# Two-pass attention: the second pass started 13 steps, not 16, behind the first

## Chip, cores, metric

The kernel runs on one core of one Trainium2 chip. The metric is the device time in microseconds (us) of one execution.

## What is computed

The reference is a chain of four blocks over an input of 8 batches of 512 rows and 128 columns, each with a residual addition and a layer normalisation: an attention with 16 heads of 8 columns and a distance bias, a gated feed-forward with block-wise quantisation, a second 16-head attention without bias, and two layers of windowed attention with a feed-forward. The change lies in the two 16-head attentions. Each of these is

```
qkv    = x @ W_qkv.T + b_qkv                     # (8, 512, 384), split in 16 heads of 8
scores = q @ k.T / sqrt(8)  (+ bias, first attention only)   # (8, 16, 512, 512)
probs  = softmax(scores)
x      = layernorm(x + (probs @ v) @ W_out.T + b_out)
```

## The kernel before

`body` runs `attention(0, ...)`, `ffn0()`, `attention(1, ...)` and `ffn1()` in that order. All is in float32 in the core's own memory, and one attention works on it batch by batch.

**Units and steps.** A batch has four units (g = 0 to 3), each of two pairs of heads. A unit needs two passes over its scores. The first pass finds the maximum of each row: for each block of 128 query rows and each pair of heads, two matmuls write scores to `s_ps`, and VectorE (DVE) reduces them to `m` (line 239). The second pass computes the scores again, transposed and with the row's maximum already subtracted, in `t_ps`; ScalarE (ACT) takes the exponential `e` (line 245); `values` multiplies by v and a column of ones, into `av`. The maximum is subtracted inside the matmul: row 63 (and 127) of the q operand holds it, against a row of -1 in the k operand. A unit takes NU = 8 steps in each pass. In the loop over steps, `step(u, i, v, k)` does step i of the first pass of one unit and step k of the second pass of an earlier one, which is LAG steps behind. So the first LAG steps hold the first pass alone, the last ones the second pass alone, and all others both.

**What hangs on the steps.** A table `todo` says which further functions run after which step; the order on TensorE (PE) is the order in which they are written, as matmuls are kept in program order. With s = 8n the first step of unit n, and z = s + LAG:

- `shift`, after step s + 9: PE transposes the maxima (`m_ps`), ACT copies them (`mt`, line 253), and GpSimd (POOL) issues two small DMAs (`q<-mt`, line 257) that put them into rows 63 and 127 of q. `t_ps` of the unit, from step z on, reads these rows.
- `values`, after steps z + 3 to z + 10; at the end ACT copies `av` to `avs` (line 274).
- `divide`, after step z + 12: PE transposes `avs` (`o_ps`), DVE divides by the sum (lines 282, 284).
- For the last unit of a batch, `end_o` after z + 15 (transpose, copy to `oT`) and `end_y` after z + 18: output projection `y_ps`, addition and statistics on DVE (lines 94 to 99), then `layernorm` on POOL (lines 104, 105, 116).
- The next batch's preparation, on the first pass's own count of steps (32 to a batch): `begin_x` after step 22, `begin_qk` after 24 (q) and 26 (k), `begin_v` after 20. `begin_qk` projects (`qk_ps`), ACT scales (lines 162, 164), POOL splits the result in two parts (`parts`, lines 167, 168), and SyncE (SP) writes them to a scratch area in DRAM (`far`, line 172). `load_qk` reads them back into the operand layout of `q` and `k` in 16 DMAs for each half of the batch (line 184), listed after steps 6, 8, 18 and 20; these write over the rows of the batch before the last one, and so wait for the last `t_ps` that reads them.

**Buffers.** q and k operands are held twice (even and odd batches). In PSUM, `s_ps` has two buffers of two banks, `av` one bank, and one pool of three banks (`p_t`) serves `t_ps` (two at each step) as well as every transpose and projection.

**Names.** A helper records the matmuls, so that PE's instructions of the attentions show as lines 126 and 127, and the tile names tell them apart.

Of the kernel before, what the change touches and what calls it, by code (L numbers as in the profile page):

```python
# [20 lines left out]
NT = S // P  # L21
# [19 lines left out]
def body(ctx, tc, x, consts, rows, wa0, wa1, acols, bo, wf, wqkv, wo, w1, w2, cols, b2r, qs, ks, out):  # L41
# [79 lines left out]
    def attention(li, alibi, qs_, ks_, late=None):  # L121
# [6 lines left out]
        with ExitStack() as st:  # L128
# [176 lines left out]
                add_and_stats(work, ps, xs, b, 0, NT)  # L305
                layernorm(work, b)

            LAG, NU = 16, 2 * NT
            todo = {}
            later = lambda s, f, *a: todo.setdefault(s, []).append((f, a))  # L310
            batch, units = [{} for _ in range(B)], []
# [480 lines left out]
    with tc.tile_pool(name="ops", bufs=1) as ops:  # L792
        qs_, ks_ = ([ops.tile([P, 8, S], F32R, name=f"{n}{i}") for i in range(2)] for n in "qk")
        for i in range(2):
            nc.vector.memset(qs_[i].bitcast(F32), 0.0)
            nc.gpsimd.memset(ks_[i].bitcast(F32), 0.0)

        def constant_rows(i, start):
            for j in range(2):
                for t, at, src in ((ks_[i], 63, rowk[16:17]), (qs_[i], 32, rowq), (ks_[i], 32, rowk[0:16])):  # L800
                    n = src.shape[0]
                    start(
                        out=t[64 * j + at : 64 * j + at + n].bitcast(F32),
                        in_=src.bitcast(F32).unsqueeze(1).broadcast_to([n, 8, S]),
                    )

        def first_late():
            constant_rows(1, held)
            load_late()

        constant_rows(0, nc.sync.dma_start)
        attention(0, True, qs_, ks_, first_late)
        for i in range(2):
            for j in range(2):
                nc.gpsimd.memset(ks_[i][64 * j + 32 : 64 * j + 48].bitcast(F32), 0.0)
        ffn0()
        attention(1, False, qs_, ks_)
# [98 lines left out]
```

## Time and profile before

| what | value |
|---|---|
| time, median of three runs | 2050.5 us (2046.76 to 2053.12) |
| profiled execution, its own time | 2052.7 us |
| its span in the profile | 2050.9 us |
| busy: PE, DVE, ACT, POOL | 1712.4, 1459.0, 1168.8, 829.0 us |
| first attention, first to last reduction `m` | 39.1 to 498.6 us |
| first attention, first to last exponential `e` | 76.5 to 521.8 us |
| second attention, first to last reduction `m` | 746.5 to 1137.7 us |
| second attention, first to last exponential `e` | 767.0 to 1157.8 us |

Busy time is the time in which an engine worked on an instruction; the profile's span runs from the first to the last instruction, and the execution's own time adds what lies around it. PEclk is the granted clock of PE in tenths. In a timeline each line has start, length, engine, source line, operation, output and inputs, shapes and number; in brackets stand the engine's idle time before it and what ended it. "SPq" is SP's queue issuing DMAs.

### The profile page before, as it was taken

Reading aid. Unit: us, or ns where it says so; the run is one execution under the profiler, and the core shown is the slowest. Engines: PE = TensorE matmul, PEld = TensorE weight load, DVE = VectorE, ACT = ScalarE, POOL = GpSimd, SP = SyncE. Lnnn points to the kernel's source line nnn. Section 1 sums busy time; section 2 is a strip of 40 time slices with the busy share of each in tenths; the row PEclk is TensorE's granted clock in tenths of the full one; section 3 lists DMA queues with packets and bytes.
Section 4 is the critical chain, followed back from the end, with each engine's and each line's share of the span. In section 5 each row is a group of like instructions: output and inputs, shape, how many; then the busy total and the mean of one; then the engine's idle time right before and its main releaser. Section 6 shows DMA issues by size and latency. Waiting matters only on the chain.

```text
span 2050.9 us, 41924 instructions
## 1 busy us (share of the span) xinstructions
PE 1712.4 (83%) x16277; PEld 981.8 (48%) x16293; DVE 1459.0 (71%) x2612; ACT 1168.8 (57%) x2749; POOL 829.0 (40%) x880
## 2 busy tenths in 40 slices
PE   1899999999476559999999757888988888888893
PEld 0445455555254424444444324556556555656562
DVE  2677777776588648888889356777777777777752
ACT  0376777777232217877778515566665566655650
POOL 3402222213445451222221434555555555666653
PEclk6699999999787659999999869999999999999997
DMA  5722222310000033333320001111111111111110
GB/s 115 185 54 64 62 52 57 64 23 2 12 1 0 0 97 79 66 65 64 71 63 2 22 16 24 30 31 33 30 32 34 33 32 32 35 35 32 29 30 21
DMA packets 91640, 88.68 MB, mean 43 GB/s; under 512 B 45825, under 2 KB 57473, under 8 KB 91442
## 3 DMA queue, kind: packets, MB, share of 16 engines
q1 hardware_dynamic: 86752, 85.00, 19.1%
q8 instruction: 129, 2.11, 0.4%
q0 software_dynamic: 4096, 0.54, 0.2%
q14 instruction: 69, 0.57, 0.1%
q10 hardware_dynamic: 594, 0.47, 0.1%
HBM read 41.33 MB, written 18.87 MB: 29 GB/s over the span
## 4 chain that ended last, share of the span: by engine, by line
PE 23%; DVE 19%; ACT 15%; POOL 3%; issue 2%; DMA 1%; SPq 1%; ACTq 0%; POOLq 0%; DVEq 0%
ACT pw L466 8%; PE av L126 6%; PE s_ps L126 5%; DVE t L567 4%; DVE r L563 4%; DVE ss L571 3%; PE t_ps L126 3%; DVE m L627 3%; ACT sq L466 2%; PE qk_ps L464 2%; ACT e L245 1%; DVE nrm L590 1%; PE qk_ps L126 1%; DVE u L742 1%; PE p_ps L465 1%
## 5 line engine op out<-in xcount | busy, mean ns | idle before, releaser
L239 DVE TENSOR_REDUCE m<-s_ps 128x2 f32<-128x1024 f32 x512 | 624.2, 1225 | 207.1 <-PE s_ps L126 203.0
L245 ACT ACTIVATE e<-t_ps 128x512 f32<-128x512 f32 x1024 | 555.8, 595 | 185.4 <-PE t_ps L126 175.2
L126 PE MATMUL av<-e,va 128*32 128x256 f32 x4096 | 328.6, 393 | 10.4 <-ACT avs L274 10.3
L466 ACT ACTIVATE pw<-sp,m,nrm 128x128 f32<-128x128 f32 x512 | 226.5, 461 | 183.7 <-DVE m L629 183.0
L126 PE MATMUL s_ps<-k,q 63*128 63x512 f32 x1024 | 266.9, 515 | 48.3 <-DMA k<-far 24.0
L126 PE MATMUL t_ps<-q,k 64*128 64x512 f32 x1024 | 249.0, 449 | 0.0
L257 POOL DMA_DIRECT2D q<-mt x128 | 68.4, 538 | 437.7 <-ACT mt L253 437.7
L126 PEld LDWEIGHTS s_ps<-k,q 63*128 63x128 f32 x1024 | 100.3, 190 | 242.2 <-issue 153.9
L640 POOL TENSOR_TENSOR pw<-pw,den 128x1024 f32<-128x1024 f32 x64 | 121.2, 1894 | 211.3 <-DVE den L639 169.1
L574 POOL TENSOR_TENSOR r<-r,t 128x1024 f32<-128x1024 f32 x64 | 151.0, 2359 | 97.5 <-DVE t L567 95.1
L563 DVE TENSOR_TENSOR r<-qk_ps,tab 128x512 f32<-128x512 f32 x128 | 87.3, 682 | 103.0 <-ACT sq L466 103.0
L464 PE MATMUL qk_ps<-wqkv_s,hT 128*128 128x512 f32 x256 | 136.3, 659 | 16.7 <-DVE t L567 15.9
L126 PEld LDWEIGHTS t_ps<-q,k 64*128 64x128 f32 x1024 | 122.9, 189 | 20.7 <-ACT e L245 10.6
L126 PEld LDWEIGHTS av<-e,va 128*32 128x32 f32 x4096 | 81.8, 108 | 104.1 <-issue 68.8
L465 PE MATMUL p_ps<-cst,pw 128*128 128x128 f32 x512 | 76.3, 284 | 55.1 <-DVE xs L705 31.1
L466 ACT ACTIVATION_READ_ACCUMULATOR pw<-sp,m,nrm 128x1 f32 x512 | 106.1, 207 | 0.0
L126 PEld LDWEIGHTS <-sel 64*128 64x128 bf16 x2048 | 66.8, 97 | 76.4 <-issue 46.6
L467 ACT COPY v<-v_ps 128x512 f32<-128x512 f32 x64 | 37.6, 587 | 105.5 <-PE v_ps L464 105.5
L567 DVE TENSOR_TENSOR t<-qk_ps,tab 128x256 f32<-128x256 f32 x256 | 95.4, 414 | 0.0
L671 DVE COPY pT<-p_ps 128x512 f32<-128x512 f32 x128 | 84.2, 686 | 15.3 <-PE p_ps L465 14.6
L465 PEld LDWEIGHTS p_ps<-cst,pw 128*128 128x128 f32 x512 | 55.8, 142 | 72.3 <-DVE xs L705 25.3
L167 POOL CAST parts<-x 128x512 fp32r<-128x512 f32 x32 | 19.4, 607 | 170.3 <-ACT x L162 166.4
(161 smaller groups left out, 3234.3 us busy)
## 6 DMA issues: line engine op xcount, KB each, us to landing
far<-parts SPq DMA_DIRECT2D x64, 256.0 KB
q<-far SPq DMA_DIRECT2D x256, 64.0 KB
k<-far SPq DMA_DIRECT2D x256, 64.0 KB
ve<-v SPq DMA_DIRECT2D x112, 128.0 KB
xn<-in_x SPq DMA_DIRECT2D x8, 256.0 KB
q<-mt POOLq DMA_DIRECT2D x128, 4.0 KB, 2.9
hn<-xs SPq DMA_DIRECT2D x16, 128.0 KB
out<-xn SPq DMA_DIRECT2D x8, 256.0 KB
```

What stands on the lines that cost most here:

```text
L126: mm = lambda *a, **k: tc.keep_in_program_order(nc.tensor.matmul(*a, **k))
L239: nc.vector.tensor_reduce(u["m"][:, :, pp, blk], both, AX.X, ALU.max)
L245: nc.scalar.activation(e, ts[j], AF.Exp, scale=float(SLOPES[2 * vp + j]) if alibi else 1.0)
L257: nc.gpsimd.dma_start(out=q[at : at + 1, 2 * g : 2 * g + 2, :].bitcast(F32).rearrange("o a (c t) -> o (a c) t", t=P), in_=mt[8 * j : 8 * j ...
L464: mm = lambda *a, **k: tc.keep_in_program_order(nc.tensor.matmul(*a, **k))
L465: tr = lambda *a, **k: tc.keep_in_program_order(nc.tensor.transpose(*a, **k))
L466: act = lambda *a, **k: tc.keep_in_program_order(nc.scalar.activation(*a, **k))
L563: nc.vector.tensor_tensor(heads(r[:, n]), heads(ps[:, n]), cos.unsqueeze(1).broadcast_to([P, HEADS, DH]), ALU.mult)
L567: nc.vector.tensor_tensor(heads(t2[:, n])[:, :, a : a + 32], heads(ps[:, n])[:, :, 32 - a : 64 - a], sin[:, a : a + 32].unsqueeze(1).broad ...
L574: nc.gpsimd.tensor_tensor(r, r, t2, ALU.add)
L640: nc.gpsimd.tensor_tensor(pw.rearrange("p s r k -> p (s r) k"), pw.rearrange("p s r k -> p (s r) k"), den.rearrange("p s r -> p (s r)").un ...
L671: nc.vector.tensor_copy(h["pT"][:, s], ps)
```

## The change

The lag of the second pass behind the first is 13 steps instead of 16, in both attentions. All that is counted from z (values, divide, end_o, end_y) moves with it; what is counted from s stays. With 16, a multiple of the eight steps of a unit, the second pass stood at the same step within its unit as the first; with 13 it stands five steps on.

```diff
-            LAG, NU = 16, 2 * NT
+            LAG, NU = 13, 2 * NT
             todo = {}
             later = lambda s, f, *a: todo.setdefault(s, []).append((f, a))
...
             for n in range(B * G):
...
                 s, z = n * NU, n * NU + LAG
                 later(s + 9, shift, units[n])
                 later(z + 12, divide, units[n])
                 for blk in range(NT):
                     for part in range(2):
                         later(z + 2 * blk + 3 + part, values, units[n], blk, part)
```

## Prediction, made before the changed kernel ran

> **What bounds the kernel now.** I read the page first, by stages. In part 2 each digit is a fortieth of the span, 51 us. The attentions are the stretches of nines in the PE row (100 to 520 us and 780 to 1160 us), at full clock:
>
> ```profile
> PE   1899999999476559999999757888988888888893
> PEclk6699999999787659999999869999999999999997
> ```
>
> The busy time by stretches says the same in numbers (columns: stretch, its length, then busy time and instructions of PE, PEld, DVE, ACT, POOL, then clock, DMA share, GB/s):
>
> ```profile
> 100.00:500.00 400.00, 395.29 (x4901) 202.02 (x4900) 306.35 (x350) 282.33 (x544) 87.72 (x122) 1.00 0.25 50
> 499.00:522.00 23.00, 22.20 (x241) 11.48 (x245) 1.96 (x5) 18.46 (x36) 1.59 (x3) 1.00 0.01 2
> 805.00:1128.00 323.00, 319.05 (x2810) 141.07 (x2811) 278.97 (x317) 257.97 (x500) 72.44 (x108) 1.00 0.26 54
> 1138.00:1158.00 20.00, 19.26 (x173) 7.79 (x173) 2.07 (x5) 18.10 (x36) 1.15 (x2) 1.00 0.01 1
> ```
>
> PE is 99% busy wherever both passes run, so whatever makes PE wait costs its full length. The timeline gives the price of a step from one s_ps to the next: 1.47 us with both passes in the first attention (301.38, 302.85, 304.32), 1.24 us in the second (786.72, 787.96). With the first pass alone a step takes 1.13 us (DVE's reduction paces it), with the second alone 1.30 us (511.10, 512.40) and 1.09 us (exps, second attention).
>
> What decides is a chain that nothing in before waits for: the row of maxima. shift transposes it (m_ps), ACT copies it (mt), POOL issues two small DMAs (q<-mt), and t_ps of that unit, on PE, needs both. PE's timeline of one unit:
>
> ```profile
> 307.23 0.28 PE L127 MATMUL m_ps<-cst,m 128*16 128x128 f32 x1
> 307.44 0.51 PE L126 MATMUL s_ps<-k,q 63*128 63x512 f32 x2
> ...
> 309.03 0.51 PE L126 MATMUL s_ps<-k,q 63*128 63x512 f32 x2
> ...
> 310.80 0.50 PE L126 MATMUL s_ps<-k,q 63*128 63x512 f32 x2
> ```
>
> Three steps after m_ps only some 5 us have passed. How long the DMAs take varies with traffic. This is the answer on tile q, for the two issues of three units: at 409 us (nothing else moving), at 308 us and at 282 us (q and k of the next batch being loaded):
>
> ```profile
> DMA to landing us min/median/max: 1.6/1.6/1.6
> ```
>
> ```profile
> DMA to landing us min/median/max: 5.8/5.9/5.9
> ```
>
> ```profile
> DMA to landing us min/median/max: 6.5/6.6/6.7
> ```
>
> The issues come 1.1 and 1.6 us after m_ps, so the row is there 3.2 us after m_ps when quiet, 7.4 to 8.5 us when not. At lag 16, t_ps comes 10.4 us or more after m_ps in the first attention and 8.8 us in the second; the reader sees why no wait for q<-mt appears. At lag 13 it would come after about 5.
>
> POOL and SP around a batch boundary (L104 to L116 layernorm, L167 and L168 the split of q or k, L257 the row's DMAs, L172 the write to DRAM, L184 the loads):
>
> ```profile
> 266.17 0.61 POOL L167 CAST parts<-x 128x512 fp32r<-128x512 f32 x1 [13.68 <-ACT x L162]
> 266.87 1.27 POOL L168 TENSOR_TENSOR parts<-x,parts 128x512 fp32r<-128x512 f32 x1
> 268.09 1.05 POOL L257 DMA_DIRECT2D q<-mt  x2
> 271.10 0.24 POOL L104 TENSOR_SCALAR rstd<-stats 128x4 f32<-128x4 f32 x1 [1.97 <-DVE stats L99]
> ...
> 273.04 3.14 POOL L116 TENSOR_SCALAR xn<-xs,stats,rstd 128x128 f32<-128x128 f32 x4
> 276.16 1.27 POOL L168 TENSOR_TENSOR parts<-x,parts 128x512 fp32r<-128x512 f32 x1
> ```
>
> ```profile
> 277.45 1.23 SPq L172 DMA_DIRECT2D far<-parts  x2
> 278.79 3.72 SPq L184 DMA_DIRECT2D q<-far  x8
> 282.58 5.61 SPq L184 DMA_DIRECT2D k<-far  x8
> ```
>
> In before the layernorm stands behind the row's DMAs. Its place is a multiple of the lag.
>
> **What the Trainium skill says.** "DMA: Bandwidth & Descriptors", section on the anatomy of one DMA from GpSimd, gives such a DMA a fixed cost of about 2 us, nearly all completion. The quiet 1.6 us agrees; 5 to 6.7 us under load says that the fixed cost is not all. The same page, on SWDGE and HWDGE, says that a DMA engine goes round-robin between queues fed by the two, which promises that a small DMA isn't stuck behind the loads; the trace does not bear that out. "TensorE: Matmul & The Clock Gate", on the phases of a matmul, says that matmuls stay in program order, only weight loads being pulled ahead: a t_ps that waits holds all behind it. Its section on what the clock gate does lets the clock fall to half after an idle window of 3.4 us; in this trace half clock comes in multiples of 3.4 us, but also where PE was two thirds busy (69 us, first pass alone).
>
> **The change, part by part.** No instruction is added or removed; SP's order is the same. Counted in steps modulo 32 (a batch), what hangs on the lag moves three earlier: t_ps, exps and values, divide (from step 4 of 8 to 1, the step of shift), end_o (23 to 20), end_y with its layernorm (26 to 23). shift (9, 17, 25, 33), the splits (24, 26) and begin_v (20) stay.
>
> *Fill and drain.* Three steps of each single pass turn into three joint ones: 3 x (1.13 + 1.30 - 1.47) = 2.9 us and 3 x (1.13 + 1.09 - 1.24) = 2.9 us, 5.8 us if the first row is there. It isn't in the first attention: POOL's first L257 issues come at 71.59 and 72.37, behind the bias additions and splits, and the second lands at about 75.5; the first t_ps of before runs at 75.3. So nothing is won at the start, and 3 x (1.47 - 1.30) plus 0.2 is lost: +0.7. In the second the row lands at 764.0 against a t_ps at 766.2: -2.1 + 3 x (1.24 - 1.09) = -1.7. Together -1 us.
>
> *Units 0 and 1 of a batch* (shift at 9 and 17): the row lands 3.2 us after m_ps in the first; t_ps needs it after 0.2 + 3 x 1.47 + 0.4 = 5.0 us (second attention: 0.2 + 3 x 1.24 + 0.15 = 4.1). In the second, the loads that hit it start when the old rows are read for the last time, so they too come three steps earlier and are nearly through, and end_o and begin_v add 1.8 us. Zero for both, 0.5 us each at worst.
>
> *Unit 2* (shift at 25). Now POOL has layernorm, split, L257 in this order. From y_ps to L104 3.2 us (267.86 to 271.10), layernorm 4.6, split 1.9: L257 starts 9.8 us after y_ps. m_ps comes 6.4 us after y_ps (two steps, the projection 1.1, divide's transposes 0.6). So the issues are 3.4 and 3.9 us after m_ps, the second lands 2.9 us on (268.62 to 271.49, beside the same far writes): 6.8. t_ps wants it at 5.0 + 1.1 (a projection) = 6.1. PE waits 0.7 us; in the second attention m_ps is at 5.9, landing at 7.3, need 5.2: 2.1 us. Five batches have both works; in two more layernorm alone delays, costing 1.0 us each in the second. Sum 5 x 0.7 + 5 x 2.1 + 2 x 1.0 = 16 us.
>
> *Unit 3* (shift at 33, that is step 1). With layernorm gone from between L167 and L168, k is written 6.3 us after step 26 starts, not 10.6, and the loads follow; in before the traffic ends 15 us after that write, so at 21.3. m_ps comes at 14.5, the issues at 15.3 and 15.9, still in the traffic. Landing takes 5 to 6 us there (4.8 at 947 in the second attention): 6.4 to 7.2 us after m_ps, need 5.0: 1.6 us of waiting; second attention 6.1 against 4.1, 2.0. Six batches each: 6 x 3.6 = 22 us.
>
> *Clock.* The trace of before has no wait inside the joint steps. Low bound zero; at half clock a joint step took 2.6 us (82.64 to 85.23), so one 3.4 us window loses 1.5 us: I take it for six of the 24 waits, 9 us. High bound 40 us, if drops last the 17 to 20 us seen at the starts.
>
> *The rest*: divide beside shift, in one step, on three banks shared with t_ps; DVE frees o_ps 1.4 us after its start (311.69 to 313.13), next wanted after some 1.9. Zero, but before shows about 0.1 us of bank waiting a unit, so 6 us either way.
>
> Sum: -1 + 16 + 22 + 9 = +46 us on the profiled execution's 2052.7 us (span 2050.9), 2098.7; the median of the runs is 2.2 us lower, so about **2096 us**.
>
> **Rivals.** (A) *The row lands in time.* If the earlier issue relative to the loads brings landings below 4 to 5 us after m_ps, only fill and drain count: -1 to -5.8 us, and up to 6 us of bank waits, 2039 to 2051. For it: 1.6 us when quiet. It decides where traffic has ended before m_ps; my sum has it 6 us after. (B) *Waits as computed, clock falling for long*: 2110 to 2130; for it the half clock at 69 to 89 us with PE mostly busy. (C) *Half of the waits*: layernorm's delay holds, the loads are clear by unit 3: -1 + 16 = 2066, with some clock 2070. That the lag isn't changed is excluded by the instruction order.
>
> **Numbers.** Waits in both units with some clock loss 0.50 (2078 to 2108), C 0.20, B 0.15, A 0.15. 0.3%, 6 us, is about what a measurement can tell here. A splits into 0.07 faster and 0.08 within. Range 2050 to 2130.
>
> **To look for afterwards.** Right: PE's t_ps waiting for DMA q<-mt in some 20 units, by 1 to 3 us, at steps 5 and 29 of the batch; L257 behind L168 and L116; slices of PE below nine in both attentions; PEclk with gaps. Wrong: no such wait, or waits in units 0 and 1 as long as in the others; if PE stays at 99% and the time falls, A.

## The result, and the profile after

The changed kernel takes 2106.0 us (median of 6 runs, 2096.0 to 2114.1) against 2049.4 us for the kernel before beside it: **1.0273 times the time, interval 1.0248 to 1.0298**, slower. The prediction was 2096, in a range of 2050 to 2130.

The profiled execution took 2105.9 us, with a span of 2104.0 us; before it was 2050.9, so 53.1 us were lost. They lie in the attentions (first reduction `m` to last exponential `e`): the first grew from 483.8 to 495.9 us, the second from 412.5 to 451.9 us. The two feed-forward parts took the same time within 1.5 us. The page of the changed kernel, part 2, PE and its clock (in tenths) by fortieths of the span:

```profile
PE   1899999999466469999899957888988989888893
PEclk6699999999787669999999968999999999999997
```

The second attention (the nines from slice 16 on) has an eight among its PE nines, slice 20, where before it had none. Tenths of a slice are too coarse for more: its clock and the first attention show nothing here. Busy time by stretches of the changed kernel (columns as before: stretch, length, busy PE, PEld, DVE, ACT, POOL, clock, DMA share, GB/s):

```profile
100.00:490.00 390.00, 378.42 (x4631) 187.48 (x4629) 288.08 (x326) 272.02 (x518) 83.14 (x116) 0.99 0.23 51
780.00:1120.00 340.00, 316.58 (x2577) 135.75 (x2576) 254.68 (x284) 243.00 (x461) 69.64 (x102) 0.95 0.29 60
```

In the same stretches of the kernel before PE was busy 385.3 and 335.9 us, at clock 1.00. The first stretch now holds 326 DVE instructions instead of 334, the second 284 instead of 329: fewer steps were done. What PE waited for in the attentions of the changed kernel (waits: total us, times, longest):

```profile
PE t_ps L126 <- DMA q<-mt: 25.5, 24, 2.9
...
PE av L126 <- ACT avs L274: 13.6, 41, 0.5
```

The first row did not exist before. The second was 10.3 us in 46 waits. One unit 2 of the second attention (batch 3) shows where such a wait comes from. POOL's timeline of the changed kernel (L104 to L116 layernorm, L167 and L168 the split, L257 the row's DMAs):

```profile
963.71 0.23 POOL L104 TENSOR_SCALAR rstd<-stats 128x4 f32<-128x4 f32 x1 [10.99 <-DVE stats L99]
964.03 1.04 POOL L105 TENSOR_TENSOR rstd<-rstd,half 128x4 f32<-128x4 f32 x1
965.18 3.13 POOL L116 TENSOR_SCALAR xn<-xs,stats,rstd 128x128 f32<-128x128 f32 x4
968.26 0.60 POOL L167 CAST parts<-x 128x512 fp32r<-128x512 f32 x1
968.95 1.28 POOL L168 TENSOR_TENSOR parts<-x,parts 128x512 fp32r<-128x512 f32 x1
970.17 1.17 POOL L257 DMA_DIRECT2D q<-mt  x2
```

and PE's timeline in the same place:

```profile
966.68 0.28 PE L127 MATMUL m_ps<-cst,m 128*16 128x128 f32 x1
...
970.60 0.50 PE L126 MATMUL s_ps<-k,q 63*128 63x512 f32 x2
...
971.84 0.50 PE L126 MATMUL s_ps<-k,q 63*128 63x512 f32 x2
972.18 0.40 PE L126 MATMUL t_ps<-q,k 64*128 64x512 f32 x1
973.98 0.47 PE L126 MATMUL t_ps<-q,k 64*128 64x512 f32 x1 [1.41 <-DMA q<-mt]
974.38 0.64 PE L126 MATMUL av<-e,va 128*32 128x256 f32 x8
974.95 0.51 PE L126 MATMUL s_ps<-k,q 63*128 63x512 f32 x2
```

The row of maxima is ready at 967.25 (`mt` ends), but layernorm and split stand ahead of its DMAs in POOL's queue until 970.17, 3.5 us after m_ps. The second DMA lands at 973.85, and the second t_ps starts 0.13 us later. The first t_ps, which needs only the row that the first of the two DMAs brings, had started at 972.18; the two of a step, which otherwise overlap, have been torn apart. So the loss is more than the bracket shows: from s_ps to s_ps this step takes 3.11 us and the one before it 1.24, a difference of 1.87 us for 1.41 us in the bracket. Where the first t_ps of a step waits, its step is longer than the bracket says too, and a wait under 0.15 us is not listed at all. The sum at the end therefore goes by the length of steps.

Unit 3 waits without any delay on POOL. Its DMAs in batch 4 of the second attention, issued 0.9 and 1.4 us after m_ps (1037.80), beside the loads of q and k (66 GB/s in these 7 us):

```profile
DMA to landing us min/median/max: 5.3/5.5/5.6
```

Three units before, at 994.9 us with next to nothing else moving (2 GB/s):

```profile
DMA to landing us min/median/max: 1.6/1.6/1.6
```

### The profile page after: what moved, and what is told of

Its sections match the earlier page's. It is cut to its first block, busy times and chain, and to the rows that moved or that the text cites. A ratio compares the mean times of both kernels' runs of the same rounds, so it can differ in the third digit from the quotient of the medians.

```text
span 2104.0 us, 41913 instructions
## 1 busy us (share of the span) xinstructions
PE 1739.0 (83%) x16277; PEld 984.7 (47%) x16293; DVE 1458.7 (69%) x2612; ACT 1177.1 (56%) x2749; POOL 829.0 (39%) x880
## 4 chain that ended last, share of the span: by engine, by line
DVE 19%; ACT 14%; PE 13%; issue 9%; POOL 5%; DMA 3%; SPq 1%; POOLq 0%; ACTq 0%; DVEq 0%
ACT pw L466 8%; DVE t L567 4%; DVE r L563 4%; DVE ss L571 3%; DVE m L627 3%; PE av L126 3%; ACT sq L466 2%; PE s_ps L126 2%; PE qk_ps L464 2%; DMA q<-mt 2%; PE t_ps L126 2%; POOL xn L116 1%; DVE u L742 1%; DVE nrm L590 1%; ACT kT L467 1%
## 5 line engine op out<-in xcount | busy, mean ns | idle before, releaser
L126 PE MATMUL av<-e,va 128*32 128x256 f32 x4096 | 337.1, 402 | 14.6 <-ACT avs L274 14.1
L126 PE MATMUL s_ps<-k,q 63*128 63x512 f32 x1024 | 271.6, 520 | 44.3 <-DMA k<-far 23.0
L126 PE MATMUL t_ps<-q,k 64*128 64x512 f32 x1024 | 258.3, 458 | 26.1 <-DMA q<-mt 25.5
L257 POOL DMA_DIRECT2D q<-mt x128 | 68.3, 538 | 494.9 <-ACT mt L253 494.8
L467 ACT COPY v<-v_ps 128x512 f32<-128x512 f32 x64 | 37.5, 586 | 107.7 <-PE v_ps L464 107.7
L104 POOL TENSOR_SCALAR rstd<-stats 128x4 f32<-128x4 f32 x32 | 7.4, 231 | 216.7 <-DVE stats L99 169.8
```

Of the source, the lines that this page charges most:

```text
L126: mm = lambda *a, **k: tc.keep_in_program_order(nc.tensor.matmul(*a, **k))
L257: nc.gpsimd.dma_start(out=q[at : at + 1, 2 * g : 2 * g + 2, :].bitcast(F32).rearrange("o a (c t) -> o (a c) t", t=P), in_=mt[8 * j : 8 * j ...
```

## Experiments

My theory: the row of maxima comes late at two places, in unit 2 because its DMAs are issued behind layernorm, in units 1 and 3 because they land in the loads of q and k, and PE, left idle, then gets a lower clock. The rivals: the new order of the matmuls and the shared banks cost the time; or the row is merely four steps too close, whatever is ahead of it. Every experiment is an edit of the changed kernel, and ratios are to the kernel before. "Joint" steps hold both passes. "Half clock" counts the time at half clock from there to the last `e`, without the stretch at half clock in which the joint steps of each attention begin (the kernel before has one too, 69.0 to 89.5 us in the first attention); the changed kernel has 6.8 us of it in the first attention and 30.7 us in the second, the kernel before none.

**1. No row to wait for.** The second pass reads 63 rows; the row of maxima, which would be subtracted, is left out of the product. All its work (m_ps, mt, DMAs) stays.

```diff
-                        r = slice(64 * j, 64 * j + 64)
+                        r = slice(64 * j, 64 * j + 63)
```

> Lag 13, but t_ps reads 63 of the 64 rows of q and k, so that it no longer depends on the row of maxima (the subtraction of the maximum is left out; the row is still transposed, copied and moved, in the same places). Waits theory: the waits of t_ps for q<-mt (25.5 us in the changed kernel) vanish, and with them the stretches at half clock inside the attentions, and the time falls to 2040 to 2052 us, at or below the kernel before. Rival (divide and shift in one step, banks, the changed order of POOL and ACT cost the time by themselves): it stays at 2090 us or more.

Measured: 2046.9 us, 0.9993 (0.9984 to 1.0001). No t_ps waits for `q<-mt`, the joint steps have no half clock, and the attentions take 479.3 and 412.2 us. So the whole loss hangs on the row's arrival; what the order of the matmuls and the three shared banks may cost is no more than the shorter fill and drain win.

**2. The same at lag 16**, so that fill, drain and order are compared alone.

```diff
-            LAG, NU = 13, 2 * NT
+            LAG, NU = 16, 2 * NT
...
-                        r = slice(64 * j, 64 * j + 64)
+                        r = slice(64 * j, 64 * j + 63)
```

> The kernel before (lag 16) with t_ps reading 63 rows, as in e1 (the subtraction of the maximum is left out). The row is never waited for at lag 16, so this should equal the kernel before within 0.2%, and then e1 minus this is what three steps less of filling and draining are worth together with the new order, without any wait: by the prediction's formula 5.8 us less than this run. Rival (63 rows instead of 64 make t_ps itself faster): this run is some us below the kernel before, and e1's gain is partly that.

Measured: 2049.3 us, 0.9987 (0.9979 to 0.9994); attentions 481.2 and 410.9 us, joint steps as in the kernel before. Between the two kernels without the row no difference is shown by the ratios, whose intervals overlap; in the attentions of the two profiled executions lag 13 is ahead by 0.6 us, not by the 5.8 us of fill and drain. In the second attention the joint steps of lag 13 are 0.3 to 1.0 us longer in each batch from the second on; the waits of `av` for `avs`, in both attentions together, are 16.4 us at lag 13 and 10.3 at lag 16.

**3. The row's DMAs on ACT's queue** instead of POOL's.

```diff
-                    nc.gpsimd.dma_start(
+                    nc.scalar.dma_start(
```

> Lag 13, the two DMAs of the row issued from ACT's queue right after the copy to mt, not from POOL's. If POOL's layernorm and split ahead of the issue make unit 2 late (issue 3.4 us after m_ps, landing at 7.0 to 7.2), its waits (step 29 of the batch: 0.4 to 0.65 us in the first attention, 1.4 us in the second) vanish, while those of unit 3 (step 5) and of units 1 stay, since the loads are still under way: time about 2075 to 2092 us. Rival (traffic alone is what makes the row late): the waits at step 29 stay within 0.3 us of what they were and the time stays at 2096 to 2114 us. Two more issues a unit on ACT, at some 0.1 to 0.6 us each, could cost up to 10 us in the second attention.

Measured: 2070.8 us, 1.0115 (1.0097 to 1.0133). The waits for the row are gone but for 0.6 us at the start, in unit 3 too, where they had been expected to stay. SP's waits in this kernel tell why (100 to 490 us):

```profile
SPq L184 <- DMA q<-mt: 268.3, 34, 19.4
```

SP's loads now wait for the row's DMAs, so the loads are held while the row moves, and in every unit but the first its second DMA lands 3.0 to 4.2 us after m_ps. The packed trace tells why they wait, though `load_qk` has not changed: the row's DMAs, now issued by ACT, take turns with SP's on the same eight completion semaphores, and each DMA waits until the one before it on its semaphore has landed (the load issued at 289.63 us follows a row that landed at 289.61). In the changed kernel the row's DMAs have eight semaphores of their own. The loss that is left is new. ACT's timeline of this kernel:

```profile
857.48 0.25 ACT L253 CAST mt<-m_ps 16x128 fp32r<-16x128 f32 x1 [0.22 <-PE m_ps L127]
857.76 1.29 ACTq L257 DMA_DIRECT2D q<-mt  x2
859.11 2.06 ACT L245 ACTIVATE e<-t_ps 128x512 f32<-128x512 f32 x4 [1.37 <-DMA q<-mt]
```

Issuing the two DMAs takes ACT 1.29 us, in which no exponential runs, and PE now waits for `e` (7.5 us in 24 waits); the attentions take 489.8 and 433.6 us, with no half clock. The experiment moves the row out of layernorm's queue, but also shifts the loads, so it does not give layernorm's share by itself.

**4. Layernorm later**: end_y three steps on, on the step of lag 16, so that the row's issue is ahead of it.

```diff
-                    later(z + 18, end_y, b, batch[b])
+                    later(z + 21, end_y, b, batch[b])
...
-            for s in range(B * G * NU + LAG + 20):
+            for s in range(B * G * NU + LAG + 24):
```

> Lag 13, but end_y (output projection, layernorm) after z + 21, so that it stands after step 26 of the batch again, as in the kernel before, behind unit 2's row and between the two halves of k's split. Theory of two causes: unit 2's waits (step 29) vanish; but k is written to the scratch area some 4 us later, so the loads begin only 2 to 3 us before unit 3's row is issued, which then lands 6.5 to 8 us after m_ps, needing 5.0 and 4.1: waits at step 5 grow to 2 to 3 us in both attentions, with half-clock stretches, total time 2080 to 2100 us. Rival (the layernorm ahead of the row is the main cause): time falls to 2055 to 2070 us.

Measured: 2111.3 us, 1.03 (1.0267 to 1.0333), no gain and above the expected 2080 to 2100. Unit 2's waits vanish, as the mechanism says, but layernorm now sits between the splits of q and k, k is written later, and the loads run on under the rows of units 3 and 1: their waits grow to 2.2 us in the first attention and to 2.8 us in the second (both t_ps of a step together). The waits for the row total 27.8 us (25.5 in the changed kernel), half clock 47.8 us (37.5). Layernorm's place trades one unit's wait for another's.

**5. No loads**: load_qk for the second batch only; later batches compute on old q and k.

```diff
-                            later(s + 6 + 12 * part + 2 * j, load_qk, b + 1, batch[b + 1], j, part)
+                            if b == 0:
+                                later(s + 6 + 12 * part + 2 * j, load_qk, b + 1, batch[b + 1], j, part)
```

> Lag 13; the loads of q and k from the third batch on are left out (batches 2 to 7 work on the operands of batches 0 and 1; the writes to the scratch area remain). If the traffic of the loads makes the row late in units 3 and 1, the waits at steps 5 and 21 vanish, and those at step 29 (POOL's order) stay at 0.6 and 1.4 us: time about 2075 to 2090 us. Rival (loads play no part): waits at step 5 and time unchanged, 2096 to 2114 us.

Measured: 2071.7 us, 1.0114 (1.0098 to 1.0129). After the first batch's start, the waits of units 1 and 3 vanish (one of 0.18 us is left); unit 2's stay as they were, 0.55 to 0.64 us in the first attention and 1.16 to 1.42 in the second. So unit 2 waits for POOL, units 1 and 3 for the traffic. PE's timeline of this kernel at one of unit 2's waits, and, in the second fence, the busy time of the 3.4 us after it (third figure from the right: the clock):

```profile
895.90 0.40 PE L126 MATMUL t_ps<-q,k 64*128 64x512 f32 x1
897.68 0.46 PE L126 MATMUL t_ps<-q,k 64*128 64x512 f32 x1 [1.38 <-DMA q<-mt]
898.07 0.86 PE L126 MATMUL av<-e,va 128*32 128x256 f32 x8
898.86 0.80 PE L126 MATMUL s_ps<-k,q 63*128 63x512 f32 x2
```

```profile
897.60:901.00 3.40, 3.32 (x21) 1.04 (x21) 1.23 (x1) 1.48 (x3) 0.00 (x0) 0.61 0.63 164
```

The same s_ps takes 0.80 us instead of 0.50: PE is busy, and the mean clock of the stretch is 0.61. Four of the five waits of unit 2 in the second attention are followed by 3.4 us of half clock (here from 898.35 to 901.76), none of the five in the first attention (0.6 us each). The batch whose wait brought no drop is 2.1 us longer than in experiment 1, the four others 3.4 to 4.0: a drop, that is, one such stretch, costs 1.3 to 1.9 us.

**6. The same wait, filled with matmuls.** Six more matmuls ahead of unit 2's first t_ps, batches 1 to 5, second attention, on top of experiment 5.

```diff
+                    if k == 0 and not alibi and v["g"] == 2 and 1 <= v["b"] <= 5:
+                        for f in range(6):
+                            mm(
+                                ts[0], lhsT=kk[0:64, vp, vlo : vlo + P], rhs=kk[0:64, vp, :], start=True, stop=True,
+                                skip_group_check=True,
+                            )
```

> e5 (lag 13, loads from the third batch on left out) with six extra matmuls of 512 columns (some 1.4 us) ahead of the first t_ps of unit 2 in batches 1 to 5 of the second attention, the only place where e5 still waits 1.2 to 1.4 us and where four of five waits are followed by 3.4 us at half clock. If the idle PE is what drops the clock, the four stretches vanish and the second attention gets 4 to 7 us shorter than e5's 430.4 us, time about 2066 us. Rival (the clock falls for another reason): four stretches as before, same length or up to 1 us longer.

Measured: 2066.5 us, 1.0071 (1.0051 to 1.009). PE's timeline of this kernel in the same place:

```profile
894.89 1.55 PE L126 MATMUL t_ps<-k 64*128 64x512 f32 x6
896.28 0.87 PE L126 MATMUL t_ps<-q,k 64*128 64x512 f32 x2
897.08 0.64 PE L126 MATMUL av<-e,va 128*32 128x256 f32 x8
897.65 0.50 PE L126 MATMUL s_ps<-k,q 63*128 63x512 f32 x2
```

All four stretches of half clock are gone and the second attention takes 426.0 us instead of 430.4, though PE does 30 matmuls more. So it is the idle PE that lowers the clock, at 1.1 us a drop on the net and 1.0 to 2.0 by batch.

**7. A filler without removing the loads** (four matmuls, units 2 and 3, second attention, in the changed kernel).

```diff
+                    if k == 0 and not alibi and v["g"] >= 2 and 1 <= v["b"] <= 5:
+                        for f in range(4):
...
```

> Lag 13 with four extra matmuls of 512 columns (some 1 us together, written to the bank that the real t_ps overwrites) ahead of the first t_ps of units 2 and 3 in batches 1 to 5 of the second attention, where PE waits 0.9 to 2.0 us. If part of the loss is PE's clock falling to half after each wait (eight stretches, 30.6 us, in the changed kernel's second attention), PE kept busy holds the clock: fewer such stretches, time 5 to 13 us below the changed kernel's. Rival (the clock falls for another reason, or costs nothing): the same stretches, time unchanged or up to 5 us longer.

Measured: 2114.1 us, 1.0317 (1.0293 to 1.0342): the gain of 5 to 13 us did not come. Half clock in the second attention, counted without the drop in its first batch, fell from 27.3 to 17.1 us, but the waits of units 1 and 3 differed (unit 1 up to 1.77 us). With runs of the changed kernel spread over 18 us this decides nothing; experiment 6 was built without the loads for that reason.

**8. More room on both sides, at lag 13**: shift one step earlier and end_y far behind the loads.

```diff
-                later(s + 9, shift, units[n])
+                later(s + 8, shift, units[n])
...
-                    later(z + 18, end_y, b, batch[b])
+                    later(z + 36, end_y, b, batch[b])
...
-            for s in range(B * G * NU + LAG + 20):
+            for s in range(B * G * NU + LAG + 40):
```

> Lag 13 with both causes eased: shift one step earlier (after s + 8), which gives the row one step more, and end_y after z + 36 (step 9 of the batch after next step's row), so that nothing but one split stands on POOL near unit 2's row. Theory: unit 2 has no wait; unit 3 lands 5.5 to 7.5 us after m_ps and has 7.1 us in the first attention (no wait or up to 0.4) and 5.9 in the second (0 to 1.5 us). Time 2046 to 2060 us. Rival (the new order costs by itself): above 2070 us.

Measured: 2068.4 us, 1.0086 (1.0059 to 1.0113), above the 2046 to 2060 expected. Unit 2 no longer waits. In the second attention unit 3 still waits, up to 2.4 us a unit, and unit 1 up to 0.7; 10.2 us of half clock. The waits of `av` for `avs` are up as well, 20.3 us.

**9. and 10. Lags between**: 14 and 15, nothing else.

```diff
-            LAG, NU = 13, 2 * NT
+            LAG, NU = 14, 2 * NT
```

> Lag 14 in place of 13, nothing else. By the arithmetic of the prediction: end_y comes after step 24, so that layernorm and split stand ahead of unit 2's row (after step 25), which is issued 5.6 and 6.1 us after m_ps and lands about 9 us after it; t_ps (step 30) needs it after 8.2 us (first attention) and 7.0 us (second): waits of about 0.8 and 2.3 us in five batches each, more than at lag 13. Unit 3 has 7.1 and 5.9 us for a landing at 4.5 to 7.5: nearly no waits. Time 2062 to 2080 us. Rival (only the slack in steps counts): unit 2's waits shrink by a step's length too, to nothing in the first attention and 0.2 us in the second, time 2045 to 2058 us.

Measured: 2086.2 us, 1.0161 (1.0122 to 1.02), with single runs from 2071.2 to 2087.0; the expected 2062 to 2080 was missed, and the rival's 2045 to 2058 by more. Unit 2 waits 0.41 to 0.64 us in the first attention (one batch 2.17), about 1.5 in the second: one step more of slack, but layernorm moved with the lag and is still ahead of the row.

```diff
-            LAG, NU = 13, 2 * NT
+            LAG, NU = 15, 2 * NT
```

> Lag 15, nothing else. Layernorm then stands between and behind unit 2's two issues, t_ps comes 8 to 10 us after m_ps: no waits but a few tenths of a us in unit 3 of the second attention (7.1 us against landings of 5 to 7.5 us). Time 2044 to 2056 us, as before. Rival (some other cost of leaving the multiple of eight, since divide, avs and projections stand at other steps than shift): 2060 us or more without waits for q<-mt.

Measured: 2046.1 us, 0.998 (0.997 to 0.9989). The waits shown are only 0.41 us in the first attention and 2.1 in the second, with no half clock; by the length of their steps against experiment 2, the late rows of unit 3 still cost the second attention 6 us. PE waits for `avs` fell to 0.9 us; attentions 477.6 and 412.6 us.

**11. and 12. Lag 15 and lag 14 with shift a step earlier** (end_y as in the change).

```diff
-            LAG, NU = 13, 2 * NT
+            LAG, NU = 15, 2 * NT
...
-                later(s + 9, shift, units[n])
+                later(s + 8, shift, units[n])
```

> Lag 15 with shift one step earlier (after s + 8): the row gets one step more, layernorm stands behind unit 2's row and split. Theory: the 2.1 us of waits that lag 15 still had in the second attention (step 7) vanish, nothing else changes: 2040 to 2047 us. Rival (shift ahead of the maxima of its last step, or apart from divide, makes PE wait elsewhere): 2050 us or more.

Measured: 2053.0 us, 1.0009 (1.0 to 1.0019). No wait for the row in the joint steps, but the waits for `avs` are back (5.7 and 5.4 us), and lag 15's gain in the first attention is gone (484.5 and 413.8 us). The expected 2040 to 2047 was missed; the time lies in the rival's range, PE waiting elsewhere.

```diff
-            LAG, NU = 13, 2 * NT
+            LAG, NU = 14, 2 * NT
...
-                later(s + 9, shift, units[n])
+                later(s + 8, shift, units[n])
```

> Lag 14 with shift one step earlier: end_y and shift both follow step 24 and five steps lie between shift and t_ps, as at lag 15, while filling and draining are one step shorter. Unit 2's second issue stands behind layernorm's first instruction only: no waits at step 30. Unit 3 as at lag 15, a few tenths of a us in the second attention. Time 2040 to 2050 us, against 2071 to 2087 us with shift after s + 9. Rival (lag 14's cost is not unit 2's late row): 2060 us or more.

Measured: **2033.5 us, 0.9907 (0.9893 to 0.9921)**, faster than both kernels and than expected. Attentions 474.2 and 402.4 us. PE's waits of experiment 2 (lag 16 without the row):

```profile
PE av L126 <- ACT avs L274: 10.3, 46, 0.5
```

and of this kernel:

```profile
PE t_ps L126 <- DMA q<-mt: 1.3, 1, 1.3
PE av L126 <- ACT avs L274: 0.9, 2, 0.5
```

The row's one wait is the first of all, while the pipe fills. From shift to use there are six steps (seven before, four in the change); after the first batch the row is complete 3.5 to 9.6 us after m_ps, and t_ps starts 6.4 to 10.5 us after it; in two units of the second attention the step is still 0.3 to 0.4 us longer, in no other. A second gain was not expected: most batches' joint steps are 1.2 us (first attention) and 0.9 us (second) shorter than at lag 16 without the row, and nearly all waits for `avs` are gone. That these waits are the whole of the second gain isn't shown: lag 15 has as few of them, and its second attention, with unit 3's late rows and 2.3 us of waits for `x`, is no shorter than before.

## Why the prediction was right, step by step

- **Sign and mechanism** held. The 24 waits (0.15 to 2.94 us) are at steps 29 and 5 of the batch, as the prediction named them, but also at 21 and, in the first batches, 13. Experiment 1 takes them away and the loss with them; rival A, the row in time, falls. Rival C, unit 2 alone, falls with experiment 5. Rival B, long half clock, falls: the drops last 3.4 us, 6.8 at most.
- **The sum.** Experiment 1 has the same order without waiting for the row. Against it, I take the lengthening of every step, from s_ps to s_ps, in which a unit's t_ps first reads its row, and of the other steps at half clock:

| part, both attentions | predicted, us | measured, us |
|---|---|---|
| fill and drain with order and banks (-4.8), first rows late (+4.4) | -1 | -0.4 |
| unit 2 | 16 | 16.6 |
| unit 3 | 22 | 15.0 |
| unit 1 | 0 | 6.3 |
| half clock, outside these steps | 9 | 14.7 |
| all else | 0 | -0.9 |
| together | 46 | 51.5 |

- **Unit 2** was right to within 0.4 us a unit. The DMAs were issued 3.4 and 4.0 us after m_ps (predicted 3.4 and 3.9) in the first attention, 3.5 and 4.1 in the second, and landed at 7.0 (6.8) and 7.15 (7.3). The brackets show 0.4 to 0.65 us and 1.4 us, 10.0 us in ten units, but the steps are 1.1 us (0.7) and 1.9 us (2.1) longer. The two batches with layernorm alone in the second attention have no bracket, and their steps are 0.7 us longer each (1.0).
- **Unit 3** came out too high: the step that failed took one landing for all rows of an attention. In the first attention it was to be 6.4 to 7.2 us after m_ps; landings ran from 4.3 to 7.5, where the need is 5.0, and only three of the six units were clearly late, by 5.0 us together (9.6). In the second, 6.1 was expected; landings ran from 4.8 to 6.7 against a need of 4.4, and all six were late, by 10.0 us together (12).
- **Unit 1: zero predicted, 0.5 at worst.** Here the step failed that called the loads "nearly through": in the second attention landings were 5.9 to 7.5 us after m_ps against a need of 6.2, and six units were late.
- **Fill and drain.** PE waited 3.35 us for the first row (the prediction had the row late there), and 0.6 us in the second attention, where it had foreseen none. Without the row the change is worth -4.5 us in the first attention and -0.3 in the second (experiment 1 against before), with order and banks in it.
- **Clock.** Half clock adds up to 37.5 us. A joint step of the second attention takes 2.16 us in it instead of 1.24, so an estimate from these is 37.5 x (1 - 1.24 / 2.16) = 16 us. The table has 14.7, and some 3 us more lie within its waiting steps. That is nearly twice the term, because more waits dropped the clock than the six assumed (leaving out the first unit of each attention, 9 of the 10 of 1.15 us and more, none of those of 0.86 us and less), while the price, 1.5 us a drop, was met by experiments 5 and 6.
- **Luck.** That the sum for the attentions was only 5.5 us too low owes something to chance: unit 3 was 7 us too high, and the 6 us of unit 1 were missing. The clock is about what is left.
- Of what was to prove it wrong, one half came about: unit 1's longest wait, 1.42 us, is as long as unit 2's. Of what was to prove it right, the slices of PE below nine showed in the second attention alone, and the waits were 0.15 to 2.9 us, not 1 to 3.

## What to carry to other kernels

The distance between producer and consumer in a software pipeline must cover the chain at its slowest, queue and traffic included: here four steps lost 2.7%, five lost 0.9 to 1.6%, and six lost nothing on the total, though at lag 15 some rows were still late. Count where each moved item lands in every in-order queue, POOL's and SP's too, modulo the batch; a place that frees one row holds up another. When such a distance is changed, try its neighbours and the producer's step together, since the small waits of other chains move with them: the best version here was not on the line between the two kernels.

## What the runs showed of the hardware

- **Two small DMAs on POOL's queue**: 1.6 us from issue to landing when next to nothing else moved, 5.3 to 5.6 us beside the loads of q and k (66 GB/s). The prediction had quoted the Trainium skill ("DMA: Bandwidth & Descriptors", on SWDGE and HWDGE) on round-robin between queues; that this keeps a small DMA from being held up was its own reading, and the runs don't bear it out.
- **Short waits in otherwise dense work lower the clock**, mostly for 3.4 us. In the packed traces the clock changes on a grid of 3.413 us. Cut at this grid, the fourteen kernels' attentions (first to last `e`) have 3325 windows at full clock. 37 of them are followed by half clock: none of those in which PE was idle (by the ends that the profile models) for less than 0.30 of the window, all 20 with more than 0.43, and 17 of the 24 between. So what counts here is how much of a wait falls into one window, some 1.0 to 1.5 us. In the changed kernel, a wait of 1.41 us (first line) is followed by half clock (second line), while one of 2.02 us is split over two windows and none follows (columns as before):

```profile
971.90:975.32 3.42, 2.01 (x18) 0.89 (x16) 1.69 (x2) 1.75 (x4) 1.32 (x2) 1.00 0.71 176
975.32:978.73 3.41, 3.41 (x24) 0.90 (x20) 2.29 (x2) 1.73 (x4) 0.00 (x0) 0.50 0.61 178
...
1040.17:1043.58 3.41, 2.24 (x22) 0.85 (x22) 3.38 (x3) 2.17 (x4) 0.00 (x0) 1.00 0.42 70
1043.58:1046.99 3.41, 2.57 (x24) 1.14 (x25) 0.95 (x2) 1.71 (x4) 0.00 (x0) 1.00 0.00 0
```

The Trainium skill ("TensorE: Matmul & The Clock Gate", Part 1, on what the clock gate does) asks for an idle window of 3.4 us; here a window idle for about a third or more was enough, and filling the wait with matmuls removed the drop.
- **A DMA issued by ACT occupies it** for about 0.63 us (1.29 for two, experiment 3), and no exponential runs in that time.
